# Feed-forward part of a four-layer kernel: depthwise diagonals on 32x32 sixteenths of the TensorE array

## The chip, the cores and the metric

The kernel runs on one core of one Trainium2 chip. A core has five engines with a queue of instructions each: TensorE (PE, whose weight loads are shown as PEld), VectorE (DVE), ScalarE (ACT), GpSimd (POOL) and SyncE (SP, which here issues all DMAs). They work side by side and wait for one another on semaphores. The metric is the time of one execution on the device in microseconds; lower is better. All data are fp32.

## The reference

A sequence of four layers on a batch of 4 images of 64 channels and 128x128 pixels: two of them are selective scans (Mamba), one a Gabor and Fourier layer, one a pair of convolutions with a gate. The change touches only the last piece of the last layer, its feed-forward part:

```python
def pvt2ffn(t, Hh, Ww, fc1_w, fc1_b, dw_w, dw_b, fc2_w, fc2_b):
    h = t @ fc1_w.T + fc1_b                                # 64 -> 256 channels
    himg = h.transpose(0, 2, 1).reshape(Bn, Ch, Hh, Ww)
    himg = conv2d(himg, dw_w, dw_b, groups=Ch)             # 3x3, one filter a channel
    h = himg.reshape(Bn, Ch, L).transpose(0, 2, 1)
    h = jax.nn.gelu(h, approximate=False)
    return h @ fc2_w.T + fc2_b                             # 256 -> 64 channels
...
t = t + pvt2ffn(layernorm(t, ln2_w, ln2_b), ...)
return x + y                                               # y is t as an image
```

The depthwise convolution has nine taps: each output channel is the sum of nine shifted copies of its own input channel, each times one weight.

## The kernel before

The layers run one after the other, and the feed-forward part (`layer3_ffn`, from L1431) is the last. Its inputs lie in device memory: `n3`, the normalised activations, and `s3`, the sum to which the result is added. An image is cut into 8 strips of 16 rows; with 4 images there are 32 strips.

**One strip.** `first` (L1478) loads the strip's 18 rows (16 and a border row on each side) into `N`, the upper 9 rows on partitions 0 to 63 and the lower 9 on 64 to 127. A border row outside the image is set to zero by a memset on DVE (L1485, L1487). Six steps then make the 256 hidden channels as two images of 128 channels, `h1` first and then `h0`: each step is two matmuls into `ph` (L1505) and two ACT operations that write it with its bias into `h` (L1510). `ph` has one buffer of two PSUM banks. `first` is a generator: every `next(ahead)` runs one step.

The two halves of the hidden channels take different ways through the depthwise convolution.

- `h1` goes to DVE: `taps` (L1523) is one multiplication (L1532) and eight multiply-adds (L1530) over 128 partitions x 2048 elements, into `g1`. ACT applies Gelu to it (L1603).
- `h0` goes to PE: a product with a diagonal matrix of weights, one for each tap, summed in PSUM (`pd`, L1584). The diagonals are 64x64, so the array is used as four quarters, which work at the same time: for each 8 rows (`kk`), tap `k`, group of four rows `h` and half of the channels `i` there is one product from quarter row `i` to quarter column `h`. That is 2 x 9 x 2 x 2 = 72 products a strip. `pd` has two tiles with two buffers each, 4 PSUM banks. ACT applies Gelu into `g0` (L1601).

`second` (L1540) is the output projection of 8 rows into `po`, one buffer of two banks: two products with the 128 channels of `g1` (L1546), and four with 64 channels of `g0` each (L1549). DVE adds the bias and `s3`'s strip `res` (L1551), and after the second 8 rows four DMAs write the strip out (L1557).

**The order.** The loop over strips (L1564) writes down the order by hand, and `_Pin` makes the scheduler keep the order of each engine from tap to tap. Inside the taps of a strip stand, at fixed places, the steps of `first` for the next strip (after every third tap), pieces of the next strip's `taps` on DVE (`rest`, four of nine taps, then one, then four), and `second`: behind tap 3 of the first 8 rows for the strip before's second half (`owed`), and behind tap 3 of the second 8 rows for its own first half. `N` is loaded one strip ahead, `N`, `g1` and `res` have two buffers. PE, DVE, ACT, POOL and SP each run their own queue in that order.

Rows that the text names: `ph` L1505, `h` L1510, `g` L1530 and L1532, `po` L1546 and L1549, `o` L1551, `pd` L1584, `g` by Gelu L1601 and L1603. Outside the part: L826 (pixel differences in the Gabor layer, 64x64 quarters, into `pg`) and L457 (the scan's sums over states, four column tiles of 128x32, into `y`).

Of the kernel before, what the change touches and what calls it, by code (L numbers as in the profile page):

```python
# [10 lines left out]
F32 = mybir.dt.float32  # L11
# [6 lines left out]
P = 128  # L18
# [1412 lines left out]
def layer3_ffn(ctx, tc, K, w, n3, s3, out):  # L1431
# [4 lines left out]
    nc = tc.nc  # L1436
    R = 16
    HR = (R + 2) // 2
    NK = R // 8
    half = [slice(64 * h, 64 * (h + 1)) for h in range(2)]  # L1440
    cp = ctx.enter_context(tc.tile_pool(name="ffc", bufs=1))
    wp = ctx.enter_context(tc.tile_pool(name="ffw", bufs=2))
    hp = ctx.enter_context(tc.tile_pool(name="ffp", bufs=1, space=PSUM))
    dp = ctx.enter_context(tc.tile_pool(name="ffd", bufs=2, space=PSUM))
    op = ctx.enter_context(tc.tile_pool(name="ffo", bufs=1, space=PSUM))

    f1 = cp.tile([P, 2, P], F32, name="f1")
    f2 = cp.tile([P, 64], F32, name="f2")
    nc.sync.dma_start(f2, w["fc2_wT"][P:, :])

    f2h = cp.tile([P, 2, 64], F32, name="f2h")
    dwb = cp.tile([P, 2], F32, name="dwb")
    dww = cp.tile([P, 2, 9], F32, name="dww")
    diag = cp.tile([P, 9, 64], F32, name="diag")
    for h in range(2):
        nc.sync.dma_start(f1[half[h]], w["fc1_wT"].rearrange("c (t q) -> c t q", t=2))
        nc.sync.dma_start(f2h[half[h]], w["fc2_wT"][:P, :].rearrange("(i q) c -> q i c", i=2))
        nc.sync.dma_start(dwb[half[h]], w["dw_b"][:P, :].rearrange("(i q) o -> q (i o)", i=2))
    b1 = cp.tile([P, 2], F32, name="ff_fc1_b")
    nc.sync.dma_start(b1, w["fc1_b"].rearrange("(t q) o -> q (t o)", t=2))  # L1460

    g, n = (_dup(nc, cp, w[k], f"ff_{k}") for k in ("ln2_w", "ln2_b"))
    ph = hp.tile([P, 2, 4, WW], F32, name="ph", tag="ph")
    for t in range(2):
        nc.tensor.matmul(ph[:, t, 0, :1], f1[half[0], t, :], n[half[0]], start=True, stop=True)
    nc.vector.tensor_add(b1, b1, ph[:, :, 0, 0])
    nc.vector.tensor_scalar(f1, f1, g, None, ALU.mult)
    dwb1 = cp.tile([P, 1], F32, name="dwb1")
    nc.sync.dma_start(dwb1, w["dw_b"][P:, :])
    nc.sync.dma_start(dww, w["dw_w"].rearrange("(t q) k -> q t k", t=2))  # L1470
    for k in range(9):
        for h in range(2):
            nc.vector.tensor_scalar(
                diag[half[h], k, :], K.eye[half[h], half[h]], dww[half[h], 0, k : k + 1], None, ALU.mult
            )
    b2 = _dup(nc, cp, w["fc2_b"], "fc2b_")

    def first(b, r0, H):  # L1478


        nimg = n3[b].rearrange("c (r w) -> c r w", w=WW)
        N = wp.tile([P, HR, WW], F32, name="N", tag="N")
        rng = []
        if r0 == 0:
            nc.vector.memset(N[:64, 0:1, :], 0.0)  # L1485
        if r0 + R == HH:
            nc.vector.memset(N[64:, HR - 1 : HR, :], 0.0)  # L1487
        for h in range(2):
            lo, hi = r0 - 1 + h * HR, r0 - 1 + (h + 1) * HR
            a, e = max(lo, 0), min(hi, HH)  # L1490
            rng.append((a - lo, e - lo))
            nc.sync.dma_start(N[half[h], a - lo : e - lo, :], nimg[:, a:e, :])
        yield
        for t in (1, 0):
            himg = H[t] = wp.tile([P, R + 2, RW], F32, name=f"h{t}", tag=f"h{t}")
            nc.gpsimd.memset(himg[:, :, 0:1], 0.0)  # L1496
            nc.gpsimd.memset(himg[:, :, RW - 1 : RW], 0.0)
            if r0 == 0:
                nc.gpsimd.memset(himg[:, 0:1, :], 0.0)
            if r0 + R == HH:  # L1500
                nc.gpsimd.memset(himg[:, R + 1 : R + 2, :], 0.0)
            for q in range(0, HR, 3):
                ph = hp.tile([P, 2, 4, WW], F32, name="ph", tag="ph")
                for h in range(2):
                    nc.tensor.matmul(  # L1505
                        ph[:, h, :3, :], f1[half[h], t, :], N[half[h], q : q + 3, :], start=True, stop=True
                    )
                for h in range(2):
                    a, e = max(q, rng[h][0]), min(q + 3, rng[h][1])
                    nc.scalar.activation(  # L1510
                        himg[:, h * HR + a : h * HR + e, 1 : WW + 1],
                        ph[:, h, a - q : e - q, :],
                        AF.Identity,
                        bias=b1[:, t : t + 1],
                    )
                yield

    strips = [(b, r0) for b in range(B) for r0 in range(0, HH, R)]
    H = {}
    for _ in first(*strips[0], H):  # L1520
        pass

    def taps(h1):  # L1523

        g1 = wp.tile([P, R, WW], F32, name="g1", tag="g1")
        for k in range(9):
            dy, dx = divmod(k, 3)
            tap, wk = h1[:, dy : dy + R, dx : dx + WW], dww[:, 1, k : k + 1]
            if k:
                nc.vector.scalar_tensor_tensor(g1, tap, wk, g1, ALU.mult, ALU.add)  # L1530
            else:
                nc.vector.tensor_scalar(g1, tap, wk, None, ALU.mult)  # L1532
            yield g1

    def more(gen, n):
        for _ in range(n):
            g = next(gen, None)
        return g

    def second(n, g0, g1, res, o, kk):  # L1540

        b, r0 = strips[n]
        po = op.tile([P, 2, 4, WW], F32, name="po", tag="po")
        for h in range(2):
            r = 8 * kk + 4 * h
            nc.tensor.matmul(po[half[h], h], f2, g1[:, r : r + 4, :], start=True, stop=False)  # L1546
        for i in range(2):
            for h in range(2):
                nc.tensor.matmul(po[half[h], h], f2h[half[h], i, :], g0[i][half[h], kk], start=False, stop=i == 1)  # L1549
        for h in range(2):  # L1550
            nc.vector.scalar_tensor_tensor(  # L1551
                o[half[h], kk], po[half[h], h], b2[half[h]], res[half[h], kk], ALU.add, ALU.add
            )
        if kk == NK - 1:
            oimg = out[b].rearrange("c (r w) -> c r w", w=WW)
            for q in range(R // 4):
                nc.sync.dma_start(oimg[:, r0 + 4 * q : r0 + 4 * q + 4, :], o[half[q % 2], q // 2])  # L1557

    pin = _Pin(tc)
    g1 = more(taps(H[1]), 9)
    rest, owed = iter(()), None
    for n, (b, r0) in enumerate(strips):  # L1564
        simg = s3[b].rearrange("c (r w) -> c r w", w=WW)
        h0 = H[0]
        H = {}
        ahead = first(*strips[n + 1], H) if n + 1 < len(strips) else iter(())
        next(ahead, None)

        res = wp.tile([P, NK, 4, WW], F32, name="res3", tag="res3")
        for q in range(R // 4):
            nc.sync.dma_start(res[half[q % 2], q // 2], simg[:, r0 + 4 * q : r0 + 4 * q + 4, :])

        g0 = [wp.tile([P, NK, 4, WW], F32, name=f"g0{i}", tag=f"g0{i}") for i in range(2)]
        o = wp.tile([P, NK, 4, WW], F32, name="o3", tag="o3")
        for kk in range(NK):
            pd = [dp.tile([P, 4, WW], F32, name=f"pd{i}", tag=f"pd{i}") for i in range(2)]
            for k in range(9):
                dy, dx = divmod(k, 3)  # L1580
                for h in range(2):
                    r = 8 * kk + 4 * h + dy
                    for i in range(2):
                        nc.tensor.matmul(  # L1584
                            pd[i][half[h]],
                            diag[half[i], k, :],
                            h0[half[i], r : r + 4, dx : dx + WW],
                            start=k == 0,
                            stop=k == 8,
                        )  # L1590
                if k % 3 == 2:
                    next(ahead, None)
                if (kk, k) == (0, 3) and owed:
                    second(*owed)
                    more(rest, 1)
                if (kk, k) == (1, 3):
                    second(n, g0, g1, res, o, 0)
                    more(rest, 4)
                pin()
            for i in range(2):  # L1600
                nc.scalar.activation(g0[i][:, kk], pd[i], AF.Gelu, bias=dwb[:, i : i + 1])  # L1601
            if not kk:
                nc.scalar.activation(g1, g1, AF.Gelu, bias=dwb1)  # L1603
                rest = taps(H[1]) if 1 in H else iter(())
                g2 = more(rest, 4)
            pin()
        owed, g1 = (n, g0, g1, res, o, 1), g2
    second(*owed)


# [98 lines left out]
```

## Time and profile before

| | us |
|---|---|
| Median of 3 runs | 17647.88 (17646.33 to 17652.58) |
| The profiled execution, its own time | 17656.56 |
| Its span, first to last instruction | 17654.7 |
| Stretch from 16704 to 17655, the feed-forward part | 951 |
| in it, busy: PE | 912.8 |
| DVE | 745.1 |
| ACT | 334.4 |
| POOL | 15.6 |

The mean granted TensorE clock is 0.909 over the span and 0.97 in that stretch, in which the DMA engines are busy for 0.24 of the time.

The page lists the costliest groups of the whole execution; those of the feed-forward part are among the smaller. Their times in the stretch from 16750 on, by the view of groups: `pd` 4540 matmuls of 64x512 on 64*64, 600 ns each and overlapping, 619.6 us busy; `g` 248 multiply-adds of 2351 ns, 583.1 us; `h` 354 ACT operations of 582 ns; `ph` 736 matmuls; `po` 512 and 256; `o` 128 additions of 750 ns; Gelu 128 of 693 ns and 32 of 2016 ns.

How to read it: a row of a timeline or chain has the start and length in us, the engine, the line, and how many instructions are merged (x). A matmul in fp32 is two rows, and matmuls on different parts of the array overlap, so their durations are not their cost; the distance from one start to the next is. `64*128` before a shape is rows times columns of the array that the matmul uses. A bracket at the end tells how long the engine sat idle before and who released it.

### The profile page before, as it was taken

The page shows a single profiled execution, that of the slowest core. Times are in us where ns is not written, and L with a number is a line of the kernel's source. Part 1 is how long each engine was busy: PE and PEld are TensorE (multiplying, and loading weights), DVE is VectorE, ACT ScalarE, POOL GpSimd, SP SyncE. Part 2 cuts the span into 40 slices and gives each one's busy share as a digit, 9 for nine tenths or more (in the row PEclk, how much of TensorE's full clock was granted, in tenths as well). Part 3 has the DMA queues.
Part 4 walks back from the last instruction along what each step waited for, and adds up shares of the span by engine and source line. Part 5 has one row for each costly group of instructions (what it writes and reads, how often), then busy time and mean ns, then how long its engine had stood idle before and what let it go on. Part 6 is the DMA issues. An engine that isn't in the chain of part 4 may idle for free. (4 is left out here: it accounts for less than half of the span.)

```text
span 17654.7 us, 242673 instructions
## 1 busy us (share of the span) xinstructions
PE 14230.1 (81%) x82490; PEld 6984.1 (40%) x82490; DVE 15333.9 (87%) x8623; ACT 14311.2 (81%) x29985; POOL 13820.2 (78%) x7966
## 2 busy tenths in 40 slices
PE   7888888798997777777777777777777777777799
PEld 3333333387334333333333333333333333333333
DVE  8999999522216999999999999999999999999977
ACT  8999999112335999999999999999999999999733
POOL 7999999200005999999999999999999999999700
PEclk8888888799998999999999999999999999999899
DMA  6766666111212333333333333333333333333222
GB/s 160 179 179 178 175 179 177 51 61 45 72 41 79 89 90 91 88 93 85 93 85 94 83 95 84 94 86 91 87 91 86 93 87 91 89 90 91 69 59 55
DMA packets 669699, 1723.23 MB, mean 98 GB/s; under 512 B 196816, under 2 KB 232096, under 8 KB 661024
## 3 DMA queue, kind: packets, MB, share of 16 engines
q1 hardware_dynamic: 668448, 1707.69, 36.0%
q8 instruction: 646, 10.58, 0.3%
q14 instruction: 605, 4.96, 0.1%
HBM read 1434.33 MB, written 272.63 MB: 97 GB/s over the span
## 5 line engine op out<-in xcount | busy, mean ns | idle before, releaser
L632 POOL TENSOR_TENSOR ring<-ring,cb 128x1024 f32<-128x1024 f32 x5120 | 12038.9, 2381 | 335.4 <-DVE ring L626 186.1
L626 DVE TENSOR_TENSOR_SCAN ring<-da,state,bx 128x1024 f32<-128x1024 f32 x4848 | 11053.0, 2327 | 70.8 <-PE y L457 38.1
L431 ACT ACTIVATE bxT<-duT,BT 128x128 f32<-128x128 f32 x21504 | 6706.0, 389 | 29.9 <-PE bx L514 28.1
L582 ACT ACTIVATE da<-dl,A 128x1024 f32<-128x1024 f32 x5120 | 5751.0, 1139 | 168.1 <-DVE ring L626 115.2
L514 PE MATMUL bx<-cst,bxT 128*128 128x128 f32 x24576 | 3693.7, 300 | 945.1 <-DVE ring L626 641.6
L514 PEld LDWEIGHTS bx<-cst,bxT 128*128 128x128 f32 x24576 | 3248.7, 209 | 2341.9 <-DVE ring L626 1523.1
L520 PE MATMUL bx<-bc,spread 64*128 64x512 f32 (+1 forms) x8192 | 2401.2, 684 | 1439.2 <-DVE ring L626 1427.9
L457 PE MATMUL y<-ring,cst 128*32 128x512 f32 x20480 | 3030.3, 675 | 120.8 <-POOL ring L632 120.1
L526 DVE TENSOR_TENSOR bx<-du,bx 128x1024 f32<-128x1024 f32 x2048 | 2463.1, 1211 | 301.3 <-PE bx L520 183.8
L520 PEld LDWEIGHTS bx<-bc,spread 64*128 64x128 f32 (+1 forms) x8192 | 690.2, 195 | 2819.0 <-DVE ring L626 2305.6
L457 PEld LDWEIGHTS y<-ring,cst 128*32 128x32 f32 x20480 | 633.3, 119 | 2040.0 <-issue 1433.7
L1197 PE MATMUL cv<-img,cw 64*64 64x512 f32 x9216 | 1009.3, 595 | 73.2 <-DMA img<-d_x 45.5
L300 PE MATMUL bx<-S,cw 128*128 128x512 f32 x1024 | 663.2, 806 | 367.9 <-DVE ring L626 354.5
L1355 POOL MEMSET X<- 64x1 f32 x4 | 0.4, 97 | 1122.2 <-DMA cw<-in_l_conv_wT 1122.2
L435 POOL TENSOR_TENSOR bxT<-duT,BT 128x512 f32<-128x512 f32 x768 | 808.3, 1053 | 10.1 <-ACT BT L381 10.1
L1122 POOL TENSOR_TENSOR xs<-xs,cl 128x1024 f32<-128x1024 f32 x32 | 76.0, 2374 | 860.8 <-DVE cl L1121 860.8
L1496 POOL MEMSET h<- 128x18 f32 x64 | 8.3, 132 | 875.2 <-PE pd L1584 443.5
L1197 PEld LDWEIGHTS cv<-img,cw 64*64 64x64 f32 x9216 | 435.1, 134 | 645.5 <-issue 537.8
L1510 ACT ACTIVATE h<-ph,ff_fc_b 128x384 f32<-128x384 f32 (+1 forms) x384 | 201.1, 578 | 593.2 <-PE ph L1505 593.2
L1584 PE MATMUL pd<-h,diag 64*64 64x512 f32 x4608 | 632.0, 603 | 0.7 <-issue 0.7
L626 DVE TENSOR_TENSOR_SCAN ring<-da,bx 128x1024 f32<-128x1024 f32 x272 | 604.8, 2268 | 9.4 <-PE y L457 5.8
L1530 DVE SCALAR_TENSOR_TENSOR g<-h,dww,g 128x2048 f32<-128x2048 f32 x256 | 601.9, 2351 | 11.0
(314 smaller groups left out, 9963.3 us busy)
## 6 DMA issues: line engine op xcount, KB each, us to landing
cb<-c SPq DMA_DIRECT2D x5120, 128.0 KB, 2.8
dl<-d SPq DMA_DIRECT2D x2048, 128.0 KB, 3.3
du<-d SPq DMA_DIRECT2D x2048, 128.0 KB, 3.7
d<-pos SPq DMA_DIRECT2D x128, 512.0 KB, 3.7
d<-u SPq DMA_DIRECT2D x128, 512.0 KB, 3.9
X<-d_t SPq DMA_DIRECT2D x124, 256.0 KB, 4.1
S<-in_x SPq DMA_DIRECT2D x120, 256.5 KB, 4.5
res<-in_x SPq DMA_DIRECT2D x128, 128.0 KB, 3.0
```

The lines of the kernel that those rows point to most:

```text
L300: self.nc.tensor.matmul(out[: l.shape[1], k : k + 512], l, r[:, k : k + 512], start=i == 0, stop=i == len(pairs) - 1)
L431: nc.scalar.activation(t[:, k, q].rearrange("p e j -> p (e j)"), c["duT"][:, k, :], AF.Copy, scale=c["BT"][:, k, n : n + 1])
L435: nc.gpsimd.tensor_mul(t[:, k].rearrange("p q e j -> p q (e j)"), c["duT"][:, k].unsqueeze(1).to_broadcast(shape), c["BT"][:, k, NQ * g : ...
L457: nc.tensor.matmul(c["y"][DD * j : DD * (j + 1), _COLS[h]], K.sel, hc[:, _COLS[h]], start=False, stop=u["g"] == self.ng - 1,)
L514: nc.tensor.transpose(bx[:, P * m : P * (m + 1)], v["bxT"][:, m, :, :, j].rearrange("p q e -> p (q e)"), self.K.eye)
L520: nc.tensor.matmul(bx[:, _COLS[h]], self.spread[v["g"]][r], self.rows(v["c"]["B"], h, 0), start=True, stop=True)
L526: nc.vector.tensor_mul(tiles[k], v["c"]["du"][j], tiles[k])
L582: nc.scalar.activation(das[nexp], v["c"]["dl"][k], AF.Exp, scale=self.A[:, k, v["g"] : v["g"] + 1])
L626: nc.vector.tensor_tensor_scan(hs, das.pop(i), tiles[i], 0.0 if u["c"].get("reset") else st, ALU.mult, ALU.add)
L632: nc.gpsimd.tensor_mul(hc, hs, u["cb"])
L1197: nc.tensor.matmul(p[i][half[h]], W[half[i], k, :], src[half[i], at : at + 4, dx : dx + WW], start=k == 0, stop=k == 8,)
L1584: nc.tensor.matmul(pd[i][half[h]], diag[half[i], k, :], h0[half[i], r : r + 4, dx : dx + WW], start=k == 0, stop=k == 8,)
```

## The change

It rewrites `layer3_ffn` alone. The diagonals become 32x32, and the array is used as sixteen sixteenths. A product of tap `k` takes channel quarter `r` (32 partitions) and rows group `q` (four image rows), and writes PSUM bank `q` at partitions quarter `(r + q) % 4`. So the channels of bank `q` are rotated by 32 x `q`; the bias `dwb` and the projection weights `f2r` are loaded in four rotations to match. The whole strip is done at once: nine taps of 16 products, 144 in all, and `pd` is four banks with one buffer.

`second` is called once a strip, for the strip before, behind all nine taps and the Gelus: eight products of full depth 128, two additions on DVE of 128x512, four DMAs out. `taps` of the next strip is one block of nine on DVE, written down behind tap 2. The steps of `first` stand behind taps 0, 1, 2, 4, 5 and 6. `N` is loaded two strips ahead, its border memsets move to POOL; `N`, `g1` and `res` get three buffers. The setup reads more and smaller pieces (the four rotations), and makes nine diagonals of 128x32 in place of 18 of 64x64.

```diff
-    dp = ctx.enter_context(tc.tile_pool(name="ffd", bufs=2, space=PSUM))
+    quad = [slice(32 * r, 32 * (r + 1)) for r in range(NR)]     # NR = 4
+    dp = ctx.enter_context(tc.tile_pool(name="ffd", bufs=1, space=PSUM))
...
+    for b in range(NR):
+        for to, of in ((slice(32 * b, P), slice(0, P - 32 * b)), (slice(0, 32 * b), slice(P - 32 * b, P))):
+            if to.stop > to.start:
+                nc.sync.dma_start(dwb[to, b : b + 1], w["dw_b"][of, :])
+                nc.sync.dma_start(f2r[to, b, :], w["fc2_wT"][of, :])
...
+    one = cp.tile([P, 32], F32, name="one32")
+    nc.vector.tensor_reduce(one, K.eye.rearrange("p (r e) -> p e r", r=NR), AX.X, ALU.add)
+    diag = cp.tile([P, 9, 32], F32, name="diag")
     for k in range(9):
-        for h in range(2):
-            nc.vector.tensor_scalar(
-                diag[half[h], k, :], K.eye[half[h], half[h]], dww[half[h], 0, k : k + 1], None, ALU.mult
-            )
+        nc.vector.tensor_scalar(diag[:, k, :], one, dww[:, 0, k : k + 1], None, ALU.mult)
...
+    def load(m):
...
+        N = wp.tile([P, HR, WW], F32, name="N", tag="N", bufs=3)
...
-            nc.vector.memset(N[:64, 0:1, :], 0.0)
+            nc.gpsimd.memset(N[:64, 0:1, :], 0.0)
...
-    def second(n, g0, g1, res, o, kk):
...
+    def second(m, g0, g1, res, o):
+        b, r0 = strips[m]
+        po = op.tile([P, 2, 4, WW], F32, name="po", tag="po")
+        for q in range(NR):
+            nc.tensor.matmul(po[half[q % 2], q // 2], f2, g1[:, 4 * q : 4 * q + 4, :], start=True, stop=False)
+        for q in range(NR):
+            nc.tensor.matmul(po[half[q % 2], q // 2], f2r[:, q, :], g0[q], start=False, stop=True)
+        oimg = out[b].rearrange("c (r w) -> c r w", w=WW)
+        for kk in range(2):
+            nc.vector.scalar_tensor_tensor(o[:, kk], po[:, kk], b2, res[:, kk], ALU.add, ALU.add)
+            for h in range(2):
+                r = r0 + 8 * kk + 4 * h
+                nc.sync.dma_start(oimg[:, r : r + 4, :], o[half[h], kk])
...
     for n, (b, r0) in enumerate(strips):
...
+        load(n + 2)
+        ahead = first(n + 1, H)
+        res = wp.tile([P, 2, 4, WW], F32, name="res3", tag="res3", bufs=3)
...
+        for k in range(9):
+            dy, dx = divmod(k, 3)
+            for q in range(NR):
+                for r in range(NR):
+                    nc.tensor.matmul(
+                        pd[q][quad[(r + q) % NR]],
+                        diag[quad[r], k, :],
+                        h0[quad[r], 4 * q + dy : 4 * q + dy + 4, dx : dx + WW],
+                        start=k == 0,
+                        stop=k == 8,
+                    )
+            if k in (0, 1, 2, 4, 5, 6):
+                next(ahead, None)
+            if k == 2 and 1 in H:
+                g2 = taps(H[1])
             pin()
-        owed, g1 = (n, g0, g1, res, o, 1), g2
+        for _ in ahead:
+            pass
+        nc.scalar.activation(g1, g1, AF.Gelu, bias=dwb1)
+        for q in range(NR):
+            nc.scalar.activation(g0[q], pd[q], AF.Gelu, bias=dwb[:, q : q + 1])
+        if owed:
+            second(*owed)
+        pin()
+        owed, g1 = (n, g0, g1, res, o), g2
     second(*owed)
```

## The prediction

> **What bounds the kernel now.** The page first: in its 40 slices the feed-forward part is the last two, the only ones in which PE (the bottom right 99) stands above DVE (77). So I looked at that stage alone. The chain of waits over one steady strip (start, us, what):
>
> ```profile
> 17099.48 1.01 PE po L1546 x4
> 17100.49 1.43 PE po L1549 x5
> 17101.92 0.06 PE pd L1584 x2
> 17101.99 0.37 PE po L1549 x2
> 17102.36 1.72 PE pd L1584 x14
> 17104.08 0.84 PE ph L1505 x4
> 17104.92 2.74 PE pd L1584 x24
> ...
> 17112.82 1.02 PE pd L1584 x8
> 17113.84 1.01 PE po L1546 x4
> ```
>
> It is PE without a gap; the next strip's po starts at 17127.46, so a strip costs 27.98 us. Each product is two matmul rows (two passes of fp32): 24 rows in 2.74 us are six rounds of four 64x64 quarters, 0.43 us a pass at full rate (inside such runs rounds start 0.429 us apart). Then the timeline of DVE over a strip:
>
> ```profile
> 16984.17 1.29 DVE L1532 TENSOR_SCALAR g<-h,dww 128x2048 f32<-128x2048 f32 x1 [3.39 <-ACT h L1510]
> ...
> 16994.28 9.51 DVE L1530 SCALAR_TENSOR_TENSOR g<-h,dww,g 128x2048 f32<-128x2048 f32 x4
> 17004.85 1.53 DVE L1551 SCALAR_TENSOR_TENSOR o<-po,fc2b__119110,res 64x512 f32<-64x512 f32 x2 [1.05 <-PE po L1549]
> 17006.41 2.35 DVE L1530 SCALAR_TENSOR_TENSOR g<-h,dww,g 128x2048 f32<-128x2048 f32 x1
> ```
>
> The reader is to see that DVE waits in brackets for ACT's h and for po, both PE's followers: it is second. ACT is busy 10.42 us of a strip, POOL 0.56. Taps of strip 0 start at 16729.1, those of strip 31 end at 17636.2 (907.1 us), then 18.5 us of tail. Three of the strips, at image borders, take 34 to 35 us, since N's border memset (L1485, L1487) stands behind taps on DVE and ph waits for it.
>
> **The change on PE.** Depthwise: 72 products a strip on four quarters become 144 on sixteen sixteenths. Passes per sixteenth: 144 x 2 / 16 = 18, at 0.43 us 7.7 us, against 36 x 0.43 = 15.4 now. No row shows sixteen at once, so it is bounded from both sides. Nearest rows:
>
> ```profile
> 3193.48 1.03 PE L826 MATMUL pg<-m,cst 64*64 64x512 f32 x8
> 3194.34 1.03 PE L826 MATMUL pg<-h,cst 64*64 64x512 f32 x8
> 3195.20 1.03 PE L826 MATMUL pg<-h,neg 64*64 64x512 f32 x8
> ```
> ```profile
> 16506.61 1.93 PE L457 MATMUL y<-ring,cst 128*32 128x512 f32 x16
> ```
> ```profile
> 17101.34 0.64 PE L1584 MATMUL pd<-h,diag 64*64 64x512 f32 x1
> 17101.34 0.59 PE L1549 MATMUL po<-g,f2h 64*64 64x512 f32 x1
> 17101.34 0.13 PEld L1549 LDWEIGHTS po<-g,f2h 64*64 64x64 f32 x1
> 17101.34 0.19 PEld L1584 LDWEIGHTS pd<-h,diag 64*64 64x64 f32 x3
> 17101.35 0.64 PE L1584 MATMUL pd<-h,diag 64*64 64x512 f32 x1
> 17101.76 0.59 PE L1549 MATMUL po<-g,f2h 64*64 64x512 f32 x2
> ```
>
> L457 feeds four column tiles with four streams from the same partitions: 16 rows in four passes of 0.43 plus a start and an end. So four column tiles run at full rate, and so do two row tiles (L826, L1584); what is extrapolated is four row tiles with four columns. The third fence shows pd starting before po rows that precede it in the program: matmuls of free tiles pass waiting ones, which sixteen tiles need, as the second pass of each product waits for the first. But pd's tiles were free from po's start at 17100.42 and were reached only 0.9 us later, so the passing is short; from that place I estimate some eight waiting instructions. The issuer itself: at the stage's opening eight PE instructions go between two of its semaphore waits 74 ns apart (9 ns each), and load-matmul pairs start 7 ns apart; 64 instructions a tap take 0.6 us at most, under 0.86.
>
> PE's tap runs are cut by ph, and after a switch the array drains: a lone tap with four tiles is the 1.02 us row above. Sixteen add twelve pairs, 0.08: 1.10 us; two taps in a row 1.10 + 0.86. ph stands behind taps 0, 1, 2, 4, 5, 6, so there are five lone taps and two pairs: 5 x 1.10 + 2 x 1.96 = **9.4 us**. Dear end, only half of the sixteen reachable at first: a pass more per run (1.55 and 2.45), **12.7 us**. The Trainium skill's TensorE: Matmul & The Clock Gate, Part 3, states 10.6 times for sixteen 32x32 tiles at 512 columns: 16 x 0.43 / 10.6 = 0.65 a pass, 9 x 1.3 = 11.7 us, between the ends, an estimate.
>
> **A rule against it.** TensorEngine Tiling (Array Packing), Gotcha 1, says that different row tiles cannot access the same PSUM bank at the same time. Here the four row tiles of one q write one bank, in four quadrants. Under the rule only the four banks work side by side: 9 x 4 x 0.86 = 31 us. But L826 already writes one bank of pg from row tiles 0 and 64, into different halves, and starts eight rows each 0.86 us, four quarters at full rate. I take the row; the rule gives the slow rival.
>
> ph stays: 6 x 0.85 = 5.1. po: 24 rows become 16 on two column halves of full depth, 8 x 0.43 + 0.14 = 3.6 us (now 5.7). PE per strip: 9.4 + 5.1 + 3.6 = **18.1**, dear 21.4, against 27.98.
>
> **DVE.** Taps: 1.32 + 8 x 2.388 (9.51 / 4, with the gap) = 20.4. The output additions: 4 of 64x512 become 2 of 128x512, as long each since the columns are the same (0.75): 1.57 with gaps. Sum **22.0 us**, above PE's sum: DVE becomes the bound.
>
> **Waits that it adds.** Call T the end of one strip's taps on DVE. The older strip's additions follow, to T + 1.6. po has one buffer, so PE's next po waits for them: it runs T + 1.7 to 5.2, and behind it in PE's queue stand all taps of the coming strip. On ACT, g1's Gelu starts at T (2.0), the four of pd (0.69) follow to T + 4.8, before PE needs those banks. The next taps and ph then take 14.5 to 17.8 us, to T + 19.7 to 23.0; PE is due at its next po at T + 23.7. On SP, N's load for two strips on is queued behind four output DMAs (0.6 us each to issue) that wait for the additions: issued from T + 3.3 and 3.9, landed 4.2 later (N's median) at T + 8.1, where the first ph wants it at T + 6.3 to 6.8. That holds PE 1.3 to 1.8 us: it ends at T + 21.5 to 24.3. With the cheap end it all hides under DVE; with the dear end a strip becomes 22.6. ph's single buffer: ACT needs 1.2 us to empty it, a tap lies between; at most 0.3 us each for four of the six, at the cheap end only. I take 22.2. Of the order otherwise: taps for the strip after are queued on DVE once h1 is made, some 8 us before they are due; g1 and res have three buffers.
>
> **Setup and rest.** Ten more small DMAs on SP ahead of N, 0.6 us each: +6. The 18 diagonal operations (5.05 us) become ten, under N's landing: nothing. N's memset goes to POOL, idle for 98% of a strip, two strips ahead: the 20 us of border stalls go. Tail: additions 1.6, po 3.6, additions 1.6, po 3.6, additions 1.6, landing 3.1 (as now): 15 for 18.5.
>
> **Sum.** Taps 20.4, two strips without additions 40.9, 29 at 22.0 = 638: 699 for 907, so -208; setup +6; tail -3.5; 0.2 x 29 for PE's lateness +6. Together -199 from the profiled execution's 17656.6 (span 17654.7), which lies 8.7 above the median of the runs, 17647.9; taken from the median, **17449 us**, 1.1% faster.
>
> **Rivals.**
> *Sixteen tiles half used* (16%). PE's passing reaches only some eight products for good: 15.4 + 1.8 for starts, + 5.1 + 3.6 + 0.6 = 26.5 a strip, 31 x 26.5 + 20.4 = 842, -65 + 2.5: **17585**. For: the 0.9 us at 17100.42. Against: each reached product has two passes, so eight waiting ones fill sixteen tiles.
> *The bank rule holds* (10%), slower: 31 + 1.1 + 5.1 + 3.6 = 40.8, 31 x 40.8 + 20.4 = 1285, +378 + 2.5: **18028**. It turns into a loss where a strip passes 28.5, a tap 2.2 us, about six tiles at once. L826 speaks against it, with two row tiles.
> *The change does what it says and gains little* because DVE or loads bind above 22: 24 us a strip (4%) gives 17500.
> The forecast has 70%.
>
> **How the numbers follow.** Low end: no lateness, cheap setup, 17425. High: the dear PE sum with N late on it and a microsecond or so of waits unforeseen, then into the half-used case, 25.9 a strip: 17565. That leaves about 2 in 10 outside. The likeliest's own range is 17425 to 17490. 0.2% is 35 us, about what a measurement of this kernel can tell from no change. Faster: 70 + 4 + 13 of the 16; same 3; slower 10.
>
> **What would show it.** Right: pd's rows as 32*32, lone taps near 1.1 us; DVE without waits between taps of strips, start to start 22.0 to 22.5; PE's po waiting for DVE's addition, ph's first for the N load; no 34 us strips. Wrong: PE still without gaps in the chain, pd's taps over 1.6 us (half used) or near 3.4 (the bank rule); DVE waiting for ACT's h.

## The result and the profile after

The changed kernel takes **17433.82 us** (median of 4 runs, 17432.99 to 17435.54) against 17648.81 us of the kernel before beside it: ratio 0.9877, 95% interval 0.9861 to 0.9893, 215 us less. The prediction was 17449 with a range of 17425 to 17565. The profiled execution took 17435.54 us, its span is 17433.4.

The page of the changed kernel, busy tenths in 40 slices:

```profile
PE   7888888798997777777777777777777777777789
...
DVE  8999999522114999999999999999999999999999
```

In the last two slices the roles are exchanged: PE was 99 and DVE 77, now PE is 89 and DVE 99. The chain of waits of the changed kernel from 17100 to 17150 us, summed by line, agrees:

```profile
by line: DVE g L1541 80.6%; issue 9.3%; DVE o L1556 5.6%; DVE g L1543 4.8%; DVEq L1556 0.5%; DVEq L1543 0.1%; DVEq L1541 0.1%
```

No PE is left in it. (L1541 and L1543 are the taps on DVE, L1556 the output additions, L1588 the products into `pd`, L1521 `ph`, L1551 and L1553 `po`.) The timeline of the changed kernel over one strip: first rows of PE and of its weight loads (start and length in us),

```profile
17101.91 1.14 PE L1588 MATMUL pd<-h,diag 32*32 32x512 f32 x32
17103.13 0.30 PEld L1521 LDWEIGHTS ph<-N,f 64*128 64x128 f32 x4 [0.99 <-ACT h L1526]
17103.98 2.35 PE L1588 MATMUL pd<-h,diag 32*32 32x512 f32 x64
...
17120.40 0.29 PEld L1521 LDWEIGHTS ph<-N,f 64*128 64x128 f32 x2 [2.98 <-DMA N<-d_n]
...
17122.47 1.45 PE L1588 MATMUL pd<-h,diag 32*32 32x512 f32 x32
```

then DVE's, from one strip's additions to the next:

```profile
17111.72 1.41 DVE L1556 SCALAR_TENSOR_TENSOR o<-po,fc2b__119096,res 128x512 f32<-128x512 f32 x2
17113.04 1.28 DVE L1543 TENSOR_SCALAR g<-h,dww 128x2048 f32<-128x2048 f32 x1
17114.35 19.13 DVE L1541 SCALAR_TENSOR_TENSOR g<-h,dww,g 128x2048 f32<-128x2048 f32 x8
17133.40 1.40 DVE L1556 SCALAR_TENSOR_TENSOR o<-po,fc2b__119096,res 128x512 f32<-128x512 f32 x2
```

Three things are to be seen. Sixteen sixteenths work: 32 rows, a whole tap, in 1.14 us, where four quarters needed 2 x 0.86. DVE has no brackets: 1.32 us from the additions to the first tap, 1.31 to the next, then one multiply-add each 2.38, and the strip repeats after 21.68 us, 29 times within 0.07. And PE now waits. The weight loads of `ph` wait 0.99 us for ACT, but in all except the last 0.1 of these the tap before is still running. For the load of `N` they wait 2.98 us, and for 2.07 of these PE has no matmul.

Against the sum of the prediction, by the two profiled executions:

| term | predicted | measured |
|---|---|---|
| Taps of strip 0 to end of taps of strip 31 | 705 (699 + 6) for 907, -202 | 689.9 for 907.1, -217.2 |
| Setup | +6 | +4.5 (first tap 27.2 us behind the Mamba part's last step, before 22.7) |
| Tail | 15 for 18.5, -3.5 | 18.0, -0.5 |
| Sum | -199 | -213.2 |

The rest of the difference of the two executions, 8 us, lies ahead of the changed part, in code that is the same.

### The profile page after: what moved, and what is told of

It is laid out like the page before. It is cut to its first block, busy times and chain, and to the rows that moved or that the text cites. A ratio compares the mean times of both kernels' runs of the same rounds, so it can differ in the third digit from the quotient of the medians.

```text
span 17433.4 us, 251387 instructions
## 1 busy us (share of the span) xinstructions
PE 13958.2 (80%) x86842; PEld 6938.6 (40%) x86842; DVE 15273.0 (88%) x8543; ACT 14313.3 (82%) x29985; POOL 13828.3 (79%) x7974
## 5 line engine op out<-in xcount | busy, mean ns | idle before, releaser
L1197 PEld LDWEIGHTS cv<-img,cw 64*64 64x64 f32 x9216 | 481.2, 134 | 600.5 <-issue 488.4
L1541 DVE SCALAR_TENSOR_TENSOR g<-h,dww,g 128x2048 f32<-128x2048 f32 x256 | 602.1, 2352 | 11.2
L300 PEld LDWEIGHTS bx<-S,cw 128*128 128x128 f32 x1024 | 255.9, 263 | 788.0 <-DVE ring L626 464.8
```

What stands on the lines that cost most here:

```text
L300: self.nc.tensor.matmul(out[: l.shape[1], k : k + 512], l, r[:, k : k + 512], start=i == 0, stop=i == len(pairs) - 1)
L1197: nc.tensor.matmul(p[i][half[h]], W[half[i], k, :], src[half[i], at : at + 4, dx : dx + WW], start=k == 0, stop=k == 8,)
```

## The experiments

All start from the changed kernel unless said otherwise; "before" lay at 17645.0 to 17647.6 in them (one single run: 17656.7). A strip's length is the distance between two starts of `po`.

**1. The new order without the sixteenths.** 64x64 diagonals, two rotations, 72 products:

```diff
-                for r in range(NR):
+                for r in range(2):
                     nc.tensor.matmul(
-                        pd[q][quad[(r + q) % NR]],
-                        diag[quad[r], k, :],
+                        pd[q][half[(r + q) % 2]],
+                        diag[half[r], k, :],
```

> The changed kernel with its new order, but the diagonals on 64x64 quarters again (72 products a strip, rotated by 64 channels for every second bank). My theory, that the sixteenths take PE off the path and DVE binds at 21.7 us a strip: PE binds again at a lone tap of 1.88 us (1.02 + 0.86), 5 x 1.88 + 2 x 3.60 = 16.6, with ph 5.1 and po 3.6 together 25.3 us a strip, about 17550 us, so the new order alone is worth some 100 us and the sixteenths the other 115. Rival, that the order did it all and the sixteenths little: 21.7 us a strip and 17434. Rival, that the order alone brings nothing: 28 us and 17640.

Measured: 17551.41 us (17547.18 to 17554.93), ratio 0.9945 [0.993, 0.9959]; PE busy for the whole of the stage, 25.24 us in each strip. So of the 214 us some 96 come from the order, the full-depth projection and the vanished border stalls, and 118 from the sixteenths, if they are added in this order.

**2. Sixteenths without the rotation**, so that a channel quarter always writes its own quarter of the bank and only the four tiles on the array's diagonal are used:

```diff
-                        pd[q][quad[(r + q) % NR]],
+                        pd[q][quad[r]],
```

> The changed kernel with the sixteenths, but without the rotation: every product of channel quarter r writes quarter r, so that only the four tiles on the diagonal of the array are used, four at a time. Theory, that a pass costs 0.43 us per tile and what counts is how many tiles work: 9 x 4 x 0.86 = 31 us of taps, 40.8 us a strip, about 18030 us. Rival, that the issue of rows or PE's other work is what counts and the tile does not matter: near 17434.

Measured: 18027.13 us, ratio 1.0214 [1.0194, 1.0235], 40.5 us a strip, PE without a gap. Its timeline has two taps as

```profile
17101.91 7.08 PE L1588 MATMUL pd<-h,diag 32*32 32x512 f32 x64
```

that is 3.5 us each: on each of the four tiles four products follow one another, each of two passes. It is the time that the prediction's rival of the bank rule had, reached by another way: the rotation is what makes the change a gain. In the changed kernel itself all sixteen first passes start 6.7 ns apart, within 100 ns, four row tiles into one bank; that rule decides nothing here.

**3. `N` three strips ahead** (four buffers, `load(n + 3)`), so that PE no longer waits for it:

> The changed kernel with N loaded three strips ahead and in four buffers. In the trace of the changed kernel ph waits 2.4 us a strip for N, and PE's granted clock then sinks to 0.8 for some microseconds. Theory (DVE binds, this is hidden): the wait goes, the clock rises, the time stays within 0.1% of 17434 us. Rival (N's lateness is on the path, since output DMA, N, ph and taps form a ring with DVE): 30 x 2.4 = 72 us less, 17362.

Measured: 17435.81 us (17434.94 to 17437.79), ratio 0.9879 [0.9862, 0.9895]: no change. The wait for `N` is gone and another stands in its place, `po` for the addition that empties it. The views of waits from 16750 on, of the changed kernel and of this one (us in total, times, longest):

```profile
PE ph L1521 <- DMA N<-d_n: 24.6, 31, 2.1
PE po L1551 <- DVE o L1556: 52.4, 29, 6.8
```

PE's slack under DVE is used up in one place or in another. The 2.4 us a strip of the expectation is one strip, the one with the longest wait; in all, the waits for `N` are 24.6 us and not 72, which leaves the rival far less to win.

**4. What PE needs.** Six of the nine taps on DVE are left out, so that PE binds:

```diff
-        for k in range(9):
+        for k in range(3):
             dy, dx = divmod(k, 3)
             tap, wk = h1[:, dy : dy + R, dx : dx + WW], dww[:, 1, k : k + 1]
```

> The changed kernel with three of the nine taps of h1 on DVE, six left out (so g1 is another sum). DVE then has 7.5 us of work a strip. It measures PE's own bound, which I put at 18.1 to 21.4 us. From the trace of the changed kernel: five lone taps of 1.23, two pairs of 2.27, ph 5.1, po 3.6 are 19.3, and up to 2 of N's wait: 19.3 to 21.3 us a strip, 17345 to 17405 us. If PE and N's ring bound as well as DVE, it stays at 21.7 and 17420 (the first 14 us of taps saved alone).

Measured: 17369.74 us (17361.84 to 17377.65) and 19.37 us a strip, PE busy for 97% of it. In its timeline DVE is now the one that waits:

```profile
17118.70 1.41 DVE L1556 SCALAR_TENSOR_TENSOR o<-po,fc2b__119096,res 128x512 f32<-128x512 f32 x2 [5.92 <-PE po L1553]
```

PE's margin below DVE is thus 2.3 us a strip; the prediction gave it 3.9 at the cheap end.

**5. The first tap of `h1` on ACT.**

```diff
-                nc.vector.tensor_scalar(g1, tap, wk, None, ALU.mult)
+                nc.scalar.activation(g1, tap, AF.Copy, scale=wk)
```

> One part of DVE's strip moves elsewhere: the first tap of h1 (1.28 us on DVE) becomes an ACT operation. Theory: DVE binds the changed kernel (21.68 us a strip, no gap), PE's own need is 19.4, so the strip becomes 20.4 and the time falls by 31 x 1.28 = 39 us, to about 17395 us. Rival: the ring of N's load and PE's order (the po starts of the changed kernel are 19 to 25 us apart) paces the strip as well; then the time stays within 8 us of 17434. In between, if ACT's tap stands in the way of h and so of PE, a gain of 10 to 25 us.

Measured: 17397.24 us (17394.12 to 17408.83), ratio 0.9859 [0.9844, 0.9874]; DVE repeats after 20.36 us. What leaves DVE leaves the time (37 us of 39 by the medians; in the two traces, the stretch from DVE's first multiply-add to its last is 648.5 us for 688.6), which shows that DVE binds. The loads do not pace the strip.

**6. Still less on DVE**: experiments 3 and 5 together, and the output additions split between ACT and POOL.

```diff
-            nc.vector.scalar_tensor_tensor(o[:, kk], po[:, kk], b2, res[:, kk], ALU.add, ALU.add)
+            nc.scalar.activation(o[:, kk], po[:, kk], AF.Identity, bias=b2)
+            nc.gpsimd.tensor_add(o[:, kk], o[:, kk], res[:, kk])
```

> More of the same: the first tap on ACT, the output additions by ACT (bias, out of PSUM) and POOL (the strip's sum), and N loaded three strips ahead. DVE then has only eight multiply-adds, 18.9 us a strip, and PE, measured alone at 19.4 us a strip, would bind. Theory (two engines close to one another, each with its own bound): (21.68 - 19.4) x 31 = 70 us off the changed kernel, 17363 us; at most 20 us dearer if ACT's additional operations delay h. Rival: POOL's additions (128x512, no row of the trace) take several us or slow DVE, as they run beside it; then 17400 or more, and DVE's multiply-adds show over 2.40 us.

Measured: 17413.94 us (17410.1 to 17424.58), ratio 0.9868 [0.9854, 0.9883]: 51 us above the theory, and 17 above experiment 5, which left the additions on DVE. The rival came in. The chain of waits of this kernel:

```profile
17100.24 2.36 DVE g L1541
...
17102.63 3.25 DVE g L1541
...
17105.90 3.26 DVE g L1541
...
17109.19 2.36 DVE g L1541
```

and rows of its timelines of POOL, at the start of the stage, in the strip above and at the end, when DVE's taps are over:

```profile
16792.14 1.60 POOL L1557 TENSOR_TENSOR o<-o,res 128x512 f32<-128x512 f32 x1 [13.34 <-ACT o L1556]
17100.56 3.16 POOL L1557 TENSOR_TENSOR o<-o,res 128x512 f32<-128x512 f32 x1 [14.16 <-issue]
17392.12 2.49 POOL L1557 TENSOR_TENSOR o<-o,res 128x512 f32<-128x512 f32 x2 [14.38 <-ACT o L1556]
```

Two multiply-adds of each of 30 strips take 0.9 us longer, and none in any other kernel here. POOL's additions are longer too: with DVE idle one takes 1.26 us (two in 2.49), and the first layer's additions of the same size (L760, 64 of them), which the expectation overlooked, take 1.27; beside DVE's taps most take 3.2 to 3.3. The rows fit two engines that take turns. POOL's first addition, started at 17100.56, ends 1.1 us after the multiply-add that was running (17100.24 to 17102.60), and the next multiply-add lasts 3.25, 0.9 too long; then the same again. The row at 16792.14 came when the running multiply-add had only 0.5 us left, and it too ended 1.1 us behind it. So 1.8 us a strip are lost for 1.3 saved: DVE's strip is 20.83. No run takes POOL's additions alone away. Experiment 10 has this kernel's other edits (and `ph` in two tiles), with the additions on DVE, and its multiply-adds take 2.35 us on the mean against 2.57 here. ACT's share of the additions, in which it reads PSUM as in its operations for `h`, is over before the slow multiply-adds start.

**7. `N`'s border memsets back on DVE**, the load still two strips ahead:

```diff
-            nc.gpsimd.memset(N[:64, 0:1, :], 0.0)
+            nc.vector.memset(N[:64, 0:1, :], 0.0)
```

> N's border memsets go back to DVE, with N still loaded two strips ahead. The prediction put the 20 us of border stalls to this pair of edits. Theory: the lead of two strips alone hides them (the memset stands behind one strip's taps at most, and the first ph of that strip is a strip later), so the time is that of the changed kernel, 17434 within 5 us, and no strip is over 23 us. Rival: POOL was what took the stalls away; then six or so strips of 24 to 28 us and 17450 to 17460 us.

Measured: 17439.11 us (17435.69 to 17441.06), ratio 0.9882 [0.9865, 0.9898] beside 0.9877 of the changed kernel; the profiled span is 17433.5 for 17433.4, and the longest distance between two `po` 25.04 us for 25.01. The limit of 23 us for a strip was badly put, since the changed kernel's own `po` starts lie 19 to 25 us apart; what it shows is that the stalls did not come back. (The median is 5.3 us above the changed kernel's, just outside the 5 of the theory; DVE's stretch of taps is 2.0 us longer, with the memsets on it.) POOL was not needed; what is left of the pair of edits is the lead of two strips. A lead of one strip in the new order was not run.

**8. The order of products within a tap**, on the kernel of experiment 4:

```diff
-            for q in range(NR):
-                for r in range(NR):
+            for r in range(NR):
+                for q in range(NR):
```

> As e4_three_taps (six of the nine taps of h1 left out, so that PE binds: 19.37 us a strip, 17370 us), and the 16 products of a tap written in the other order: channel quarter outside, bank inside, so that four products in a row read the same partitions. Theory: the 0.2 us by which two taps in a row miss 0.86 us each is the load of the next tap's weights, one after the other, for tiles that are free; the order inside a tap does not matter and the strip stays at 19.37 within 0.2 us. Rival: the order matters, because products of one bank that follow one another are serialised at the change of tap; then the strip changes by 0.5 us or more (three pairs of taps and the last: up to 9 x 0.2 = 1.8 us shorter, 17315 us).

Measured: 17373.99 us (17368.97 to 17379.02), 19.39 us a strip: the order does not matter. That does not show the theory's cause, weight loads one after the other; why two taps in a row cost 2.27 us was left to the last experiment.

**9. `ph` in two tiles of one bank**, on the kernel of experiment 4:

```diff
-                ph = hp.tile([P, 2, 4, WW], F32, name="ph", tag="ph")
+                ph = [hp.tile([P, 4, WW], F32, name=f"ph{h}", tag="ph", bufs=2) for h in range(2)]
```

> As e4_three_taps (six of the nine taps of h1 left out, so that PE binds: 19.37 us a strip, 17370 us), with ph as two tiles of one bank in place of one of two banks: a step's first product then waits for the older step's first ACT operation alone. Theory: of the 2.07 us that a lone tap and its step take together, 0.1 to 0.2 are the wait for ACT; five or six such places a strip make the strip 18.5 to 18.9, the time 17345 to 17355. Rival: PE changes from ph to pd and back at that price anyway, by the draining of the array; then the strip stays at 19.2 to 19.4 and ph's first loads wait for the pass before them instead of ACT.

Measured: 17349.7 us (17348.19 to 17351.22), 18.97 us a strip. So 0.40 us of PE's 19.37 are the price of the single buffer of `ph`, which ACT has to empty; a little less than the theory's 0.5 to 0.9.

**10. Experiments 3, 5 and the two `ph` tiles together:**

> e5_first_tap_act with N three strips ahead and ph in two tiles: DVE keeps eight multiply-adds and two additions, 20.36 us a strip, and everything that delays PE is taken away. Theory: DVE alone sets the time, so it is that of e5_first_tap_act, 17397, within 8 us. Rival: PE's stalls for N still cost e5 something at its ends (start and last strips); then 17380 to 17388.

Measured: 17396.04 us (17391.13 to 17402.65), ratio 0.9859 [0.9843, 0.9876], DVE 20.36 us a strip. PE's waits for `N` and for `ph`'s single buffer were taken away, and the time is that of experiment 5. These two are faster than both kernels of the case, by some 250 us and 37 us.

**11. Why a run of taps costs more than its passes.** First the changed kernel's view of weight loads for a pair of taps with 16 tiles:

```profile
17103.97 0.23 PEld L1588 LDWEIGHTS pd<-h,diag 32*32 32x32 f32 x32 [0.55 <-issue]
17104.43 0.10 PEld L1588 LDWEIGHTS pd<-h,diag 32*32 32x32 f32 x1 [0.23 <-issue]
17104.86 0.55 PEld L1588 LDWEIGHTS pd<-h,diag 32*32 32x32 f32 x31 [0.33 <-issue]
```

The first tap's 32 loads go at once. While its second passes run, a single load of the second tap goes (at 0.46 us), and the other 31 only at 0.89. The experiment thins the pairs out:

```diff
-                for r in range(NR):
+                for r in range({3: 3, 4: 3, 7: 2, 8: 2}.get(k, NR)):
...
-                        stop=k == 8,
+                        stop=k == (8 if r < 2 else 6),
```

> Measures what makes a run of taps dearer than 0.86 us each. The changed kernel with fewer products in the two pairs of taps: three of the four channel quarters in taps 3 and 4 (12 tiles), two in taps 7 and 8 (8 tiles); those products are left out of h0's convolution. In the changed kernel, with 16 tiles, one weight load of the second tap goes 0.46 us after the first tap's start, the other 31 only at 0.88. Theory, an instruction window of 64 that is freed in order (the Trainium skill, TensorE: Matmul & The Clock Gate, Part 3, The mechanism, has a 64-deep reorder window): at 0.46 us the oldest unfinished instruction is the second pass of the first product, the fourth instruction of the tap, so the window ends 64 further on: with 16 tiles (64 instructions a tap) it reaches the first product of the next tap alone, one load; with 12 tiles (48 a tap) five products, five loads at 0.46 us; with 8 tiles (32 a tap) all eight. The pair of 8 tiles then takes about 1.8 us in place of 2.35, that of 12 in between. Rival: loads go strictly in order, one product after the other, or the loading of many small tiles is slow by itself; then one load goes at 0.46 us in both and the pairs take 2.2 to 2.35 us. The time as a whole stays at 17434 within 10 us in either case, since DVE sets it.

Measured: 17436.77 us in one run. Its weight loads, the pair with 12 tiles and then the pair with 8:

```profile
17105.61 0.20 PEld L1588 LDWEIGHTS pd<-h,diag 32*32 32x32 f32 x24 [0.55 <-issue]
17106.07 0.13 PEld L1588 LDWEIGHTS pd<-h,diag 32*32 32x32 f32 x5 [0.25 <-issue]
17106.50 0.42 PEld L1588 LDWEIGHTS pd<-h,diag 32*32 32x32 f32 x19 [0.30 <-issue]
...
17112.83 0.18 PEld L1588 LDWEIGHTS pd<-h,diag 32*32 32x32 f32 x16 [0.54 <-issue]
17113.29 0.15 PEld L1588 LDWEIGHTS pd<-h,diag 32*32 32x32 f32 x8 [0.28 <-issue]
17113.72 0.15 PEld L1588 LDWEIGHTS pd<-h,diag 32*32 32x32 f32 x8 [0.28 <-issue]
```

Five and eight loads, in all of the 28 strips looked at. From the pair's start to the next row of PE it is 2.15 us with 12 tiles and 1.88 with 8, against 2.27 with 16. The three counts fit a window counted from the oldest instruction that has not ended (at 0.46 us the second pass of the first product, the fourth instruction of the tap): they put its depth between 62 and 65, and the 64 of the expectation lies among these. A tap on sixteen tiles in fp32 is 64 instructions (16 products, each of two weight loads and two matmuls), so the window holds one tap and hardly more. (Every product here is four instructions, so a limit of 17 products would give the same counts.)

## Why the prediction was right, and where its sizes were off

**What bounds before, and that DVE takes over: right.** Experiment 4 gives PE 19.4 us a strip, the timeline gives DVE 21.68, and experiment 5 shows that only what DVE loses is won. The 87% for faster rested on this.

**"Sum 22.0 us" for DVE: measured 21.68, and the term that was mis-sized is the additions.** Charged were 1.57 us for the two; they take 1.32 to the start of the next tap, because neighbouring operations overlap (two of 745 ns are 1.41 together, and the tap begins before they end). That is 0.25 of the 0.32 us a strip. The taps were right within 0.07 (1.32 + 8 x 2.388 predicted, 1.31 + 8 x 2.38 measured). 0.32 a strip is 9 us.

**"I take 22.2": the 0.2 us of lateness did not come**, 6 us. The dear end for it assumed that PE ends late in a strip; PE's margin of 2.3 us is enough for all its waits. These two terms are the 15 us between prediction and result in the stretch of taps. Setup and tail were off as well, by 1.5 us one way and 3.0 the other, which in part cancels by chance.

**PE's sum, 18.1 us (dear 21.4): measured 19.37.** It splits as follows. Two taps in a row were put at 1.96 and take 2.27, twice a strip: 0.62. The single buffer of `ph` was put at "at most 0.3 us each for four of the six": 0.40 in all (experiment 9). The other 0.25 are small excesses, such as 1.14 for the lone tap's 1.10. The nine taps together take 5 x 1.14 + 2 x 2.27 = 10.2 us; charged were 9.4, and the estimate from the factor of 10.6 was 11.7. The forecast did not need these, since they are hidden; with DVE at 18.9 us they would decide.

**"Some eight waiting instructions": wrong.** The estimate came from one place of the trace in which `pd` was reached 0.9 us after its tiles were free. In the changed kernel the sixteen first passes start within 100 ns, the last of them ahead of fifteen waiting second passes, and the window is some 64 deep (experiment 11). The forecast held because its cheap end leaned on full use, and the half-used rival (16%) had this estimate as its only ground. What held `pd` back at 17100.42 stays open: its first product for a free tile stands some 20 instructions behind the oldest that had not ended, well inside such a window.

**The bank rule (10%): not seen**, in the changed kernel four row tiles start into each of four banks within 100 ns, and a tap takes 1.14 us where the rule made it 3.4. **The rival of 24 us a strip** falls with experiments 3 and 7: neither the loads nor the memsets pace anything.

**The waits: the one for `N` was there, in most strips shorter than thought, and hidden as said.** Predicted were 1.3 to 1.8 us a strip. The strip shown, the longest, has 2.07 on its first load and 0.33 on the next; over the stage it is 24.6 us in 31 waits, some 0.8 a strip. The sign that "PE's `po` waits for DVE's addition" is all but missing in the changed kernel until the last strips: `N`'s wait delays PE so that the addition is done when it comes. Experiment 3 brings that wait out. What was not in the sum is the clock. The changed kernel's windows (us, busy time of PE, PEld, DVE, ACT and POOL, then the granted clock, DMA share and GB/s):

```profile
17117.00:17121.00 4.00, 1.93 (x36) 0.53 (x34) 3.96 (x2) 0.00 (x0) 0.00 (x0) 1.00 0.94 227
17123.20:17126.50 3.30, 3.30 (x52) 0.78 (x36) 3.23 (x3) 1.46 (x4) 0.00 (x0) 0.50 0.02 5
17126.60:17130.00 3.40, 3.40 (x84) 1.15 (x68) 3.37 (x2) 1.06 (x3) 0.00 (x0) 1.00 0.00 0
```

Some 3 us after a stretch of 2.07 us without a matmul the granted clock halves, for 3.4 us, and the lone tap at 17122.47, which runs into that time, takes 1.45 us for 1.14. (The 0.8 in the expectation of experiment 3 is a mean over a window that holds both values.) Ten such stretches of 3.4 or 6.8 us lie between 16750 and 17345; what sets them off was not worked out. They too hide under DVE in the middle of the stage.

**The tail: "15 for 18.5" was 18.0.** There the clock is on the path. PE has no work for the 8.5 us in which DVE ends the last strip's taps, and then:

```profile
17408.40:17413.20 4.80, 0.00 (x0) 0.00 (x0) 4.73 (x3) 0.00 (x0) 0.00 (x0) 1.00 0.00 0
17416.80:17420.10 3.30, 3.21 (x8) 1.11 (x10) 0.00 (x0) 2.97 (x5) 0.00 (x0) 0.50 0.71 164
17420.20:17424.00 3.80, 2.21 (x12) 0.69 (x10) 1.41 (x2) 0.00 (x0) 0.00 (x0) 1.00 0.41 129
```

At half the clock the first `po` is over 5.3 us after its start (17416.89 to 17422.18, when the addition starts) in place of 3.6, and the span ends 4.5 us after the last addition in place of 3.1. **Setup** was 4.5 us for 6.

**The border stalls went, for half of the reason given.** The prediction named POOL and the two strips together; experiment 7 shows that in the new order the lead is enough.

## What to carry to other kernels

Where a change speeds one engine up beyond the next, the gain is set by the second engine's own sum, to be made from starts of neighbouring operations and not from their lengths; what the first engine then waits for costs nothing until that sum shrinks. Small array tiles pay only if products that follow one another fall on different tiles in both directions (the rotation is worth 590 us here), and a batch that just fills PE's window of some 64 instructions repeats at 1.08 us for 0.86. Before work is moved from a full DVE to an idle POOL, a run has to show that the two do not hold each other up (experiment 6).

## What the runs showed of the hardware

- Sixteen 32x32 tiles with four row tiles writing each bank run side by side: first passes start 6.7 ns apart, second passes 454 ns behind them. A single tap is through in 1.14 us; in a long row of taps (288 rows in 9.75 us) it is 1.08 us a tap, as it would be with a window that is freed in order. The Trainium skill (TensorE: Matmul & The Clock Gate, Part 3, The mechanism) states the 64; the loads of 1, 5 and 8 with 16, 12 and 8 tiles agree with it and add the order of freeing.
- POOL additions of 128x512, 1.26 us alone, take 3.2 to 3.3 us beside DVE's multiply-adds, and lengthen one of these each from 2.36 to 3.25 us. The Trainium skill (SBUF — State Buffer, Who interferes with whom) says that a DVE operation with two SBUF inputs contends with a GpSimd operation that reads SBUF, and that what they share is locked by one of them at a time. The trace agrees, and shows the turns to be whole instructions: POOL's addition ends 1.1 us after the running multiply-add does, and the next one is 0.9 us late.
- In the trace of the changed kernel the granted clock is 1.00 or 0.50 and nothing between. It was 0.50 for 3.4 us, beginning 2.8 us after a gap of 2.07 us between matmuls had ended, and for 6.8 us, beginning 4.9 us into a gap of 8.5 us.
